# A Transformer expert layer: the products of v and W of two pairs taken together in seven block products

## The chip, the cores and the metric

The kernel runs on one core of a Trainium2 chip. The metric is the device time of one execution in microseconds. The engines are named as in the profile: PE (matrix products, with PEld for loading their stationary operand), DVE (vector engine), ACT (scalar engine, functions of one operand), POOL (GpSimd) and SP (here only a queue that issues DMAs). PE writes its results to eight PSUM banks of 512 columns of fp32; DVE and ACT read them there. Everything is in fp32.

## The reference, cut to what matters

x has 8 rows (batches) of 512 tokens of 256 values; each row has 64 context vectors and one anchor vector.

```python
nx = layer_norm(x, ln_gamma, ln_beta)
q = nx @ Wq
k = prototype_bank @ Wk
v = prototype_bank @ Wv
weights = softmax(einsum('bth,bph->btp', q, k) * H ** (-0.5))
evidence = einsum('btp,bph->bth', weights, v)
combined = concatenate([nx, evidence, anchor], axis=-1)        # 3 x 256 wide
router_probs = softmax(combined @ router_W + router_b)          # 3 experts
h = silu(einsum('btc,ecr->bter', combined, e_w1) + e_b1)        # 512 hidden values an expert
expert_out = einsum('bter,erh->bteh', h, e_w2) + e_b2
routed = sum(expert_out * router_probs[..., None], axis=-2)
g = sigmoid(silu(combined @ gate_w1 + gate_b1) @ gate_w2 + gate_b2)
return x + g * (routed @ out_w + out_b)
```

The kernel uses that `evidence @ W = weights @ (v @ W)`, where W is the middle third of an expert's first-layer weights. So it needs, for each row, the small product of v (64 x 256) and W (256 x 512 for each of three experts, and 256 + 2 columns for gate and router).

## The kernel before

The 8 rows are taken in 4 pairs, 0 to 3. A pair's two rows of v are stacked to 128 rows, so that one product of v and W serves both. A pair passes through three stages:

- `gate_layer(j, within)`: the first layer of the gate. Seven products of the two rows' x stand for eight (a block scheme after Strassen and Winograd, in which the two rows of a pair and the two halves of the contraction are the blocks). `within` is a table of further steps, run at named points (1, 5, 6, 3, "sums", 7, each after the product of that number).
- `half_layers(j)`: the first layers of the experts, written out by hand in `SLOTS` (pairs 1 to 3) and `SLOTS_0` (pair 0). A slot holds two half products, which run side by side on the two halves of PE's rows, and steps for other engines: `k` keeps a sum from PSUM, `a` adds one, `s` is silu, `w` weighs with the router's probabilities, `df` is a difference, `vw` the differences of v and W that the block scheme needs, `st`, `nm`, `lg`, `xd`, `xg` prepare x of the next pair.
- `outputs(j, between)`: the gate's second layer, then the second layers of the experts, again in block products (`experts`, six products of 512 columns each, into banks u, y, z), with `subtract` between them for the block differences and `keep` and `finish` to add the sums up. `finish` is three DVE operations (add the bank, multiply by the gate, transpose to `yb`), one POOL addition of x, and the stores on SP. `between` is a table of steps for the next pair, run at the points "begin", "gate", P1, P5, P6, P2, P7, P3, P4 in this order. Among these: `transpose_blocks` (x of one row by 32x32 blocks on DVE, then scaled on ACT), `scores` (PE), `exponents` (DVE, then eight exponentials on ACT), `combine_x` (four block differences of x, on POOL), `softmax`, `evidence_logits`, `router_logits` and `turn_weights` (DVE), `router_exp` (ACT).

The whole program is issued in the order in which it is written (`tc.manual_schedule(engines=None)`): each engine runs its instructions in that order, and waits are set where an operand, a tile or a bank is not yet free. So a step that is put at another point moves in every queue it uses.

`value_weights(j, g)` takes the product of v and W of pair j for expert g (or for gate and router, g = E): two products of 512 columns into a bank (L820), a copy by ACT into the tile `vw` (L827), and `value_differences` by DVE (L834, on 64 rows). In pairs 1 to 3 the steps stand at "begin" (gate and router), P6 (expert 2) and P7 (expert 0) of the outputs before, and at point 3 of the gate layer (expert 1, whose difference is the step `vw` in the half layers' first slot).

The block `pb` of router probabilities is spread over all rows by POOL's DMAs: four writes `pd` from the transposed probabilities to DRAM and one broadcast back (L800, L804), issued at the start of the half layers and first used by step `w00.2` in slot 17. The add behind it, `a10.2`, reads bank 5, into which slot 21 opens a new sum (`U.4`).

Lines that the text uses: L845 all products that go through `product`, L691 scores, L670 and L610 transposing and scaling of x, L682 `combine_x`, L705 to L719 `exponents` (L706 the copy of the first scores, L707 the clearing of them, L717 the maximum, L719 the exponentials), L735 and L736 `softmax`, L887 and L890 adding and keeping sums in the first layers, L921 and L924 `df` and `w`, L1300 `subtract`, L1330 to L1333 `finish` (L1333 is POOL's addition).

Of the kernel before, what the change touches and what calls it, by code (L numbers as in the profile page):

```python
# [8 lines left out]
F32 = mybir.dt.float32  # L9
AF = mybir.ActivationFunctionType  # L10
ALU = mybir.AluOpType
# [5 lines left out]
def kernel(  # L17
# [51 lines left out]
    nc = tc.nc  # L69
    P = 128  # L70
    B, T, H = x.shape
    CT = context.shape[1]
    E, C3, RH = e_w1.shape
    KH = H // P
# [7 lines left out]
    NP = B // 2  # L82
# [3 lines left out]
    const = ctx.enter_context(tc.tile_pool(name="const", bufs=1))  # L86
# [13 lines left out]
    def bank(i, name):  # L100
        ps = psum.tile([P, 512], F32, tag=f"b{i}", name=name)
        bank_of[ps.name] = i
        return ps
# [129 lines left out]
    w1 = const.tile([P, 2 * KH, R0 + ED], F32, tag="w1", name="w1")  # L233
# [53 lines left out]
    vT = const.tile([P, KH, B * CT], F32, tag="vT", name="vT")  # L287

    mr = const.tile([P, KH, B, CT], F32, tag="mr", name="mr")
# [206 lines left out]
    ow_sb = const.tile([P, KH, H], F32, tag="ow_sb", name="ow_sb")  # L496
# [79 lines left out]
    S = {}  # L576
# [47 lines left out]
    def logits(j):  # L624

        if ("lg", j) not in S:
            S["lg", j] = work.tile([P, E, NJ], F32, tag="lg", name=f"lg_{j}")
            nc.gpsimd.memset(S["lg", j][:, 0, :], 0.0)
        return S["lg", j]
# [70 lines left out]
    def exponents(j):  # L700
        ps = S.pop(("ps_s", j))
        w = work.tile([P, 2, NJ, TB], F32, tag="w", name=f"w_{j}", bufs=1)
        S["w", j] = w
        tokens = w.rearrange("p g j c -> p j g c")
        nc.vector.transpose(w.rearrange("p g j c -> p (g j c)"), ps)  # L705
        nc.vector.tensor_copy(logits(j)[:, 1, :], w[:, 0, :, 0])  # L706
        nc.vector.memset(w[:, 0, :, 0], 0.0)  # L707
        mx = work.tile([P, NJ], F32, tag="mx", name=f"mx_{j}")
        nc.vector.tensor_reduce(mx, tokens, AX.XY, ALU.max)
        sm = work.tile([P, NJ], F32, tag="sm", name=f"sm_{j}")  # L710
        S["sm", j] = sm
        if j == 0:
            nc.vector.tensor_tensor(w, w, by_token(mx), ALU.subtract)
            nc.scalar.activation(w, w, AF.Exp, scale=SCALE)
            return
        nmx = work.tile([P, NJ], F32, tag="nmx", name=f"nmx_{j}")
        nc.vector.tensor_scalar_mul(nmx, mx, -SCALE)  # L717
        for t in range(NJ):
            nc.scalar.activation(  # L719
                w[:, :, t, :], w[:, :, t, :], AF.Exp, bias=nmx[:, t : t + 1], scale=SCALE,  # L720
                accum_out=sm[:, t : t + 1],
            )
# [6 lines left out]
    def by_token(a):  # L729
        return a.unsqueeze(1).unsqueeze(3).to_broadcast([P, 2, NJ, TB])  # L730
# [80 lines left out]
    def value_weights(j, g, copy=nc.scalar.copy, whole=True):  # L811


        if ("vw", j) not in S:
            S["vw", j] = work.tile([P, R0 + ED], F32, tag="vw", name=f"vw_{j}", bufs=1)
        n0, n1 = (g * RH, (g + 1) * RH) if g < E else (G0, R0 + ED)
        vw = S["vw", j][:, n0:n1]
        ps = misc(f"ps_vw_{j}_{g}")[:, : n1 - n0]
        for k in range(KH):
            nc.tensor.matmul(  # L820
                ps,
                vT[:, k, j * 2 * CT : (j + 1) * 2 * CT],
                w1[:, KH + k, n0:n1],
                start=(k == 0),
                stop=(k == KH - 1),
            )
        copy(vw, ps)  # L827
        if whole and g < E:
            value_differences(j, g)

    def value_differences(j, g):
        odd = S["vw", j][CT:, g * RH : (g + 1) * RH]
        odd = odd.rearrange("p (q i c) -> p q i c", i=2, c=P)
        nc.vector.tensor_tensor(odd[:, :, 0, :], odd[:, :, 0, :], odd[:, :, 1, :], ALU.subtract)  # L834

    GROUPS = (NE // 2, *range(NE // 2))
    U, Z, Y = {}, {}, {}
# [3 lines left out]
    def product(ps, lhsT, rhs, start=False):  # L843

        return nc.tensor.matmul(ps, lhsT, rhs, start=start, stop=True, skip_group_check=not start)  # L845
# [80 lines left out]
    def gate_layer(j, steps):  # L926
# [63 lines left out]
        "P7.4 Z.6 | s10.3 w11.3 k10.6",  # L990
        "P2.4 P1.5 | w10.3",
        "P4.3 P5.5 | df.1 k00.5 df.3",
        "U.3 P2.4 |",
        "P5.6 Z.5 | a00.4",
        "P6.5 P4.3 | s00.4 k11.6 w00.4",
        "P7.6 Z.4 | s01.3",
        "P5.5 P6.5 | w01.3",
        "P2.5 P7.6 | k10.5 k11.5",
        "Y.5 P3.6 | a11.6",
        "Y.6 P7.4 | s11.6 w11.6",  # L1000
        "P7.5 P5.4 |",
        "P4.6 V.5 |",
        "P5.4 P7.5 |",
        "U.6 P3.5 | k11.4 a11.5",
        "P2.6 V.6 | a11.4 s11.5 s11.4 w11.5",
        "P3.5 P2.5 | w11.4",
# [92 lines left out]
    def half_layers(j):  # L1099
# [23 lines left out]
        def half(token, k):  # L1123
# [12 lines left out]

        b0 = 2 * j + 2
        simple = {
            "vw": lambda: value_differences(j, 1),
            "r": lambda: (router(j), spread_probabilities(j)),  # L1140
            "xb0": lambda: load_x_blocks(2 * j),
            "xb1": lambda: load_x_blocks(2 * j + 1),
# [8 lines left out]
            **{f"l{e}": lambda e=e: load_second(e) for e in range(1, E)},  # L1151
            **{f"t{u}": lambda u=u: transpose_second(u) for u in range(2 * E)},
        }
        ahead = {
            "dev": lambda: [deviation(j + 1, i) for i in range(2)],
            "xd0": lambda: store_x(b0),
# [78 lines left out]
    def outputs(j, steps):  # L1235
# [20 lines left out]
        t2, t3, t4 = gate_sums.pop(j)  # L1256
        g1, g2, g22 = scratch_x("r11"), scratch_x("r12"), scratch_x("r22")
        u, z, y = (bank(i, f"ps_g{n}_{j}") for n, i in (("u", 0), ("z", 2), ("y", 4)))
# [33 lines left out]
        def subtract(dst, other):  # L1292

            (k, i), (k2, i2), (k3, i3) = dst, *other
            for e in range(E):
                d, p, m = (
                    S["h", ii, e].rearrange("p (q k) t -> p q k t", k=2)[:, :, kk, :]
                    for kk, ii in ((k, i), (k2, i2), (k3, i3))
                )
                nc.vector.tensor_tensor(d, p, m, ALU.subtract)  # L1300
# [14 lines left out]
        def keep(r, ps):  # L1315
            nc.vector.tensor_tensor(r, r, ps, ALU.add)
# [42 lines left out]
        u, y, z = (bank(i, f"ps_{n}2_{j}") for i, n in ((1, "u"), (3, "y"), (5, "z")))  # L1359
# [5 lines left out]
        experts(z, combo(S1), 0, 1, start=True)  # L1365
        subtract((0, 1), ((1, 1), (0, 1)))
        keep(r22, z)
        subtract((0, 0), ((0, 1), (0, 0)))
        run("P5")
        experts(u, combo(S2), 0, 1)  # L1370
# [52 lines left out]
        y = work.tile([P, NT, P], F32, tag="yb", name="y_rows")  # L1423
# [4 lines left out]
    with tc.manual_schedule(engines=None):  # L1428
# [84 lines left out]
        for j in range(NP):  # L1513


            within, between = {}, {}

            def put(where, n, step, *args):
                where.setdefault(n, []).append(lambda: step(*args))

            spares(7, 5)
            if j == 0:
                spares(4, 5, 1)
                copies = []

                def value_product(g):
                    value_weights(0, g, lambda *args: copies.append(args), False)

                def copy_values():
                    nc.scalar.copy(*copies.pop(0))  # L1530

                put(within, 1, value_product, 0)
                put(within, 1, begin_softmax)
                put(within, 5, copy_values)
                put(within, 6, load_table, AF.Silu)
                put(within, 3, value_product, 1)
                put(within, 3, copy_values)
                put(within, "sums", end_softmax)
                put(within, 7, value_product, 2)
                put(within, 7, copy_values)  # L1540
                put(within, 7, end_setup)
            else:
                put(within, 3, value_weights, j, 1, nc.scalar.copy, False)
            if j + 1 < NP:
                b0, b1 = 2 * j + 2, 2 * j + 3
                if j + 2 < NP:
                    put(between, "begin", load_x, b0 + 2)
                    put(between, "begin", load_x, b1 + 2)
                put(between, "begin", transpose_blocks, b0)
                put(between, "gate", regroup_x, b1)  # L1550
                put(between, "begin", value_weights, j + 1, E)
                put(between, "begin", store_router_rows, j + 1)
                put(between, "begin", spread_router_rows, j + 1)
                put(between, "P5", transpose_blocks, b1)
                put(between, "P6", value_weights, j + 1, 2)
                put(between, "P2", scores, j + 1)
                put(between, "P2", exponents, j + 1)
                put(between, "P2", combine_x, j + 1, nc.gpsimd)
                put(between, "P7", softmax, j + 1)
                put(between, "P7", value_weights, j + 1, 0)  # L1560
                put(between, "P7", evidence_logits, j + 1)
                put(between, "P7", router_logits, j + 1)
                put(between, "P3", turn_weights, j + 1)
                put(between, "P3", router_exp, j + 1)
            gate_layer(j, within)
            half_layers(j)
            outputs(j, between)


# [32 lines left out]
```

## Time and profile before

| | |
|---|---|
| median of 3 runs (lowest to highest) | 457.83 us (457.56 to 457.87) |
| profiled execution, its time | 456.89 us |
| its span | 455.0 us |
| gate layer of pair 1, half layers | from 142.3, from 149.3 us |
| outputs of pair 1 | 198.4 to 247.0 us |
| gate layer of pair 2, half layers | from 247.0, from 254.0 us |
| outputs of pair 2 | 303.1 to 351.7 us |
| gate layer of pair 3, half layers | from 351.7, from 358.7 us |
| outputs of pair 3 | from 407.8 us |

In the profile an instruction's line names the line of the kernel, the engine and operation, what it writes and reads (`out<-in`, by the program's names), the shape and how many are merged. In a timeline the first two columns are start and duration in microseconds; a bracket at the end gives the time for which the engine had been idle before it and which instruction ended that idle time. Products overlap in their records: the duration of one is longer than the distance to the next, so the distance between starts is what a product costs. A product of fp32 shows as two records.

### The profile page before, as it was taken

The page shows a single profiled execution, that of the slowest core. Times are in us where ns is not written, and L with a number is a line of the kernel's source. Part 1 is how long each engine was busy: PE and PEld are TensorE (multiplying, and loading weights), DVE is VectorE, ACT ScalarE, POOL GpSimd, SP SyncE. Part 2 cuts the span into 40 slices and gives each one's busy share as a digit, 9 for nine tenths or more (in the row PEclk, how much of TensorE's full clock was granted, in tenths as well). Part 3 has the DMA queues.
Part 4 walks back from the last instruction along what each step waited for, and adds up shares of the span by engine and source line. Part 5 has one row for each costly group of instructions (what it writes and reads, how often), then busy time and mean ns, then how long its engine had stood idle before and what let it go on. Part 6 is the DMA issues. An engine that isn't in the chain of part 4 may idle for free.

```text
span 455.0 us, 5502 instructions
## 1 busy us (share of the span) xinstructions
PE 450.1 (99%) x1797; PEld 214.5 (47%) x1797; DVE 360.2 (79%) x683; ACT 214.0 (47%) x373; POOL 99.1 (22%) x149
## 2 busy tenths in 40 slices
PE   8999999999999999999999999999999999999996
PEld 7544445754444444444444444444444444444445
DVE  2878999949599899579699999479879747677983
ACT  3545875563221675466221576468220446558000
POOL 6466600252081300001072300001053400000010
PEclk9999999999999999999999999999999999999999
DMA  8984672354012477203011277002011381000014
GB/s 263 385 165 122 95 250 34 61 123 50 1 23 39 107 192 141 57 0 47 7 23 23 48 239 125 8 1 46 7 23 23 55 208 18 1 0 0 1 17 75
DMA packets 119379, 35.31 MB, mean 78 GB/s; under 512 B 106012, under 2 KB 116312, under 8 KB 118840
## 3 DMA queue, kind: packets, MB, share of 16 engines
q1 hardware_dynamic: 115344, 27.02, 28.9%
q0 software_dynamic: 2080, 7.16, 4.7%
q10 hardware_dynamic: 1928, 0.80, 0.7%
q8 instruction: 14, 0.23, 0.2%
q14 instruction: 13, 0.11, 0.1%
HBM read 27.56 MB, written 7.39 MB: 77 GB/s over the span
## 4 chain that ended last, share of the span: by engine, by line
PE 98%; DMA 1%; ACT 0%; DVE 0%; ACTq 0%; issue 0%
PE ps_u L845 45%; PE ps_z L845 20%; PE ps_y L845 14%; PE ps_vw L820 5%; PE ps_gu L845 3%; PE ps_w2o L547 2%; PE ps_s L691 2%; PE ps_gz L845 2%; PE ps_tokens L845 1%; PE ps_v L356 1%; DMA scr_w<-in_L_xcond_Wk_dram 1%; PE ps_m L356 1%; PE ps_gy L845 1%; PE pt_x L619 0%; PE ps_kq L369 0%; PE ps_ar L456 0%
## 5 line engine op out<-in xcount | busy, mean ns | idle before, releaser
L845 PE MATMUL ps_u<-nxT,w 64*128 64x512 f32 (+1 forms) x208 | 96.5, 590 | 0.0
L924 DVE TENSOR_TENSOR h<-h,pb 128x512 f32<-128x512 f32 x96 | 62.6, 684 | 16.3 <-ACT h L881 11.1
L845 PE MATMUL ps_u<-h,w2o 128*128 128x512 f32 x144 | 64.2, 595 | 0.0
L881 ACT ACTIVATE h<-h,abias 128x512 f32<-128x512 f32 x72 | 49.1, 717 | 29.8 <-DVE h L887 29.8
L845 PE MATMUL ps_z<-wT,vw 64*128 64x512 f32 x104 | 52.3, 590 | 0.0
L845 PE MATMUL ps_y<-nxT,w 64*128 64x512 f32 (+1 forms) x104 | 51.6, 590 | 0.0
L845 PE MATMUL ps_z<-nxT,ws 64*128 64x512 f32 (+1 forms) x104 | 51.5, 591 | 0.0
L845 PE MATMUL ps_z<-T,ws 64*128 64x512 f32 (+1 forms) x104 | 51.5, 590 | 0.0
L1333 POOL TENSOR_TENSOR yb<-yb,xb 128x512 f32<-128x512 f32 x14 | 17.7, 1267 | 149.0 <-DVE yb L1332 131.9
L845 PEld LDWEIGHTS ps_u<-nxT,w 64*128 64x128 f32 (+1 forms) x208 | 37.5, 187 | 25.6 <-issue 23.1
L845 PE MATMUL ps_u<-T,ws 64*128 64x512 f32 (+1 forms) x104 | 49.4, 589 | 0.0
L845 PE MATMUL ps_u<-T,w 64*128 64x512 f32 x112 | 48.3, 589 | 0.0
L845 PE MATMUL ps_z<-h,w2s 128*128 128x512 f32 x96 | 42.5, 592 | 0.0
L845 PEld LDWEIGHTS ps_u<-h,w2o 128*128 128x128 f32 x144 | 27.0, 190 | 32.6 <-issue 30.9
L890 ACT COPY h<-ps_u 128x512 f32<-128x512 f32 x48 | 27.8, 580 | 22.7 <-PE ps_u L845 22.7
L1300 DVE TENSOR_TENSOR h<-h,h 128x1024 f32<-128x1024 f32 x24 | 34.3, 1484 | 0.0
L433 POOL DMA_DIRECT2D vrd<-vw x8 | 5.0, 629 | 114.2 <-ACT vw L827 111.6
L845 PEld LDWEIGHTS ps_z<-h,w2s 128*128 128x128 f32 x96 | 18.2, 190 | 23.0 <-issue 21.8
L845 PE MATMUL ps_u<-wT,vw 64*128 64x512 f32 x56 | 28.3, 594 | 0.0
L845 PE MATMUL ps_y<-wT,vw 64*128 64x512 f32 x56 | 28.2, 595 | 0.0
L820 PE MATMUL ps_vw<-w,vT 128*128 128x512 f32 (+1 forms) x64 | 26.7, 539 | 0.0
L845 PEld LDWEIGHTS ps_y<-nxT,w 64*128 64x128 f32 (+1 forms) x104 | 19.4, 187 | 13.1 <-issue 12.8
(231 smaller groups left out, 817.1 us busy)
## 6 DMA issues: line engine op xcount, KB each, us to landing
pb<-pd POOLq DMA_DIRECT2D x4, 1536.0 KB, 6.9
xb<-in_x_dram SPq DMA_DIRECT2D x64, 64.0 KB, 2.5
out_dram<-yb SPq DMA_DIRECT2D x56, 64.0 KB, 1.8
x<-in_x_dram SPq DMA_DIRECT2D x24, 128.0 KB, 2.9
xd<-x SPq DMA_DIRECT2D x24, 128.0 KB, 2.3
xg<-xd SPq DMA_DIRECT2D x48, 64.0 KB, 2.3
w<-in_L_xcond_e_w_dram SPq DMA_DIRECT2D x4, 512.0 KB, 7.4
scr_wa<-in_L_xcond_e_w_dram SPq DMA_DIRECT2D x3, 512.0 KB, 10.2
```

The costliest lines, as they stand in the source:

```text
L356: nc.tensor.matmul(ps, w_sb[:, k, m * P : (m + 1) * P], src[:, k, :], start=(k == 0), stop=(k == KH - 1))
L433: nc.gpsimd.dma_start(S["vrd", j][i].rearrange("e c -> c e"), S["vw", j][row_half(i), R0:])
L547: nc.tensor.matmul(ps[:, d * H : (d + 1) * H], w2["T"][u % 2][:, c : c + P], ow_sb[:, k, :], start=(k == 0), stop=(k == KH - 1),)
L691: nc.tensor.matmul(ps[side(i, h), g * NH : (g + 1) * NH], mr[:, k, 2 * j + i, g * TB : (g + 1) * TB], S["nxT", 2 * j + i][:, k, h * NH : ( ...
L820: nc.tensor.matmul(ps, vT[:, k, j * 2 * CT : (j + 1) * 2 * CT], w1[:, KH + k, n0:n1], start=(k == 0), stop=(k == KH - 1),)
L845: return nc.tensor.matmul(ps, lhsT, rhs, start=start, stop=True, skip_group_check=not start)
L881: nc.scalar.activation(h, h if src is None else src, AF.Silu, bias=abias[:, c, 2 * j + i : 2 * j + i + 1])
L890: nc.scalar.copy(chunk(n, i, d), part)
L924: nc.vector.tensor_tensor(h, h, S["pb", j][:, i, :, 2 * q // RC, :], ALU.mult)
L1300: nc.vector.tensor_tensor(d, p, m, ALU.subtract)
L1333: nc.gpsimd.tensor_tensor(yb, yb, S["xb", 2 * j + row][:, i, :], ALU.add)
```

## The change

The products of v and W of pairs 2 and 3 are no longer taken one pair at a time. v of the two pairs and W of two experts (or the two halves of one) are 2 x 2 blocks each, and seven products of blocks stand for eight. Part 0 takes experts 0 and 1 (512 columns a product) in the outputs of pair 1; part 1 takes the two halves of expert 2 (256 columns) in the gate layer of pair 2. Each part has four steps (`late_values`):

- first: product 1 into bank u, product 2 into bank y; ACT copies u to c11, DVE adds y;
- second: product 6 is added into u; ACT copies u to c12;
- third: product 7 is added into u, product 5 goes into z; ACT copies z to c22, DVE adds u to it;
- fourth: product 4 is added into u, ACT copies u to c21; product 3 is added into z, DVE adds z to c12; then `value_differences`.

c11 and c12 are columns of pair 2's `vw`, c21 and c22 those of pair 3, which now lies in the tile of the first-layer weights, `w1`, in the rows of W that are no longer needed. Part 0's steps stand at P5, P6, P7 and P3, after the steps that stood there, part 1's at points 1, 5, 6 and 7 of the gate layer.

The block differences are taken by DVE: those of W for part 0 in four slots of pair 1's half layers (`v0` to `v3`), those of v in another (`vs`), those of W for part 1 at P4 of pair 1's outputs, which is after the last `finish`. Their homes are tiles that are free by then (`ow_sb`, part of `mr`, parts of `vT`, of `w1`, and one new tile).

Besides, for all pairs: the second row's `transpose_blocks` moves from P5 to a new point P8, between the `keep` of z and the subtraction that stood behind it; `scores`, `exponents` and `combine_x` move from P2 to P6, ahead of what else stands there; from pair 1 on, the copy of the first scores in `exponents` is done by ACT instead of DVE. Pair 3's `value_differences` come at P7, P3 and in the first slot of its half layers; pair 2 has none in that slot.

```diff
-        nc.vector.tensor_copy(logits(j)[:, 1, :], w[:, 0, :, 0])
+        (nc.scalar.copy if j else nc.vector.tensor_copy)(logits(j)[:, 1, :], w[:, 0, :, 0])
...
-        if ("vw", j) not in S:
+        if ("vw", j) not in S and j > JS:
+            S["vw", j] = w1[:, KH, :]
+        elif ("vw", j) not in S:
...
+    JS = NP - 2
+    late_v = {}
+
+    def block_rows(n):
+
+        ctx_of = [slice((JS + i) * 2 * CT, (JS + i + 1) * 2 * CT) for i in range(2)]
+        v = [[vT[:, k, ctx_of[i]] for k in range(KH)] for i in range(2)]
+        free = [vT[:, k, i * P : (i + 1) * P] for k in range(KH) for i in range(2)]
+        if n is None:
+            (a11, a12), (a21, a22) = v
+            s1, s2, s4, s3 = free
+            for dst, p, m, op in (
+                (s1, a21, a22, ALU.add), (s2, s1, a11, ALU.subtract),
+                (s3, a11, a21, ALU.subtract), (s4, a12, s2, ALU.subtract),
+            ):
+                nc.vector.tensor_tensor(dst, p, m, op)
+            return None
+        return {
+            1: v[0][0], 2: v[0][1], 3: free[2], 4: v[1][1], 5: free[0], 6: free[1], 7: free[3],
+        }[n]
+
+    def block_columns(part):
+
+        if part not in late_v:
+            if part == 0:
+                c0, n = 0, RH
+                t4 = const.tile([P, RH], F32, tag="late_t4", name="late_t4")
+                late_v["t4"] = t4
+                ts = ow_sb.rearrange("p k n -> p (k n)"), mr[:, :, : B // 2, :], t4
+            else:
+                c0, n = 2 * RH, RH // 2
+                ts = ow_sb[:, 0, :], ow_sb[:, 1, :], late_v["t4"][:, :n]
+            w = [
+                [w1[:, KH + k, c0 + i * n : c0 + (i + 1) * n] for i in range(2)] for k in range(KH)
+            ]
+            late_v[part] = w, ts
+        return late_v[part]
...
+    def late_difference(part, n):
+        ((b11, b12), (b21, b22)), ts = block_columns(part)
+        t1, t2, t4 = (t.rearrange("p k b c -> p k (b c)") if len(t.shape) > 3 else t for t in ts)
+        dst, p, m = ((t1, b12, b11), (t2, b22, t1), (b12, b22, b12), (t4, b21, t2))[n]
...
+    def late_product(part, n, ps, start=False):
+
+        ((b11, b12), (b21, b22)), ts = block_columns(part)
+        t1, t2, t4 = (t.rearrange("p k b c -> p k (b c)") if len(t.shape) > 3 else t for t in ts)
+        rhs = {1: b11, 2: b21, 3: b22, 4: t4, 5: t1, 6: t2, 7: b12}[n]
+        product(like(ps, rhs), block_rows(n), rhs, start)
+
+    def late_homes(part):
+        (c0, n) = (0, RH) if part == 0 else (2 * RH, RH // 2)
+        first, second = S["vw", JS], w1[:, KH, :]
+        return [a[:, c0 + i * n : c0 + (i + 1) * n] for a in (first, second) for i in range(2)]
+
+    def late_values(part, banks):
+
+        n = RH if part == 0 else RH // 2
+        u, y, z = (bank(i, f"ps_late_{m}")[:, :n] for i, m in zip(banks, "uyz"))
+
+        def plus(dst, ps):
+            nc.vector.tensor_tensor(dst, dst, ps, ALU.add)
+
+        def first():
+            c11 = late_homes(part)[0]
+            late_product(part, 1, u, True)
+            nc.scalar.copy(c11, u)
+            late_product(part, 2, y, True)
+            plus(c11, y)
+
+        def second():
+            late_product(part, 6, u)
+            nc.scalar.copy(late_homes(part)[1], u)
+
+        def third():
+            c22 = late_homes(part)[3]
+            late_product(part, 7, u)
+            late_product(part, 5, z, True)
+            nc.scalar.copy(c22, z)
+            plus(c22, u)
+
+        def fourth():
+            late_product(part, 4, u)
+            nc.scalar.copy(late_homes(part)[2], u)
+            late_product(part, 3, z)
+            plus(late_homes(part)[1], z)
+            for g in (0, 1) if part == 0 else (2,):
+                value_differences(JS, g)
+
+        return first, second, third, fourth
...
-        "U.3 P2.4 |",
+        "U.3 P2.4 | v0",
...
-        "P2.5 P7.6 | k10.5 k11.5",
+        "P2.5 P7.6 | k10.5 k11.5 vs",
...
-        "P7.5 P5.4 |",
-        "P4.6 V.5 |",
-        "P5.4 P7.5 |",
+        "P7.5 P5.4 | v1",
+        "P4.6 V.5 | v2",
+        "P5.4 P7.5 | v3",
...
-            "vw": lambda: value_differences(j, 1),
+            "vw": lambda: [value_differences(j, g) for g in ((1,) if j < JS else () if j == JS else (2,))],
...
+        for n in range(4):
+            simple[f"v{n}"] = lambda n=n: late_difference(0, n) if j == JS - 1 else None
+        simple["vs"] = lambda: block_rows(None) if j == JS - 1 else None
...
         keep(r22, z)
+        run("P8")
         subtract((0, 0), ((0, 1), (0, 0)))
         run("P5")
...
-            else:
+            elif j < JS:
                 put(within, 3, value_weights, j, 1, nc.scalar.copy, False)
+            elif j == JS:
+                for point, step in zip((1, 5, 6, 7), late_values(1, (6, 5, 7))):
+                    put(within, point, step)
...
-                put(between, "P5", transpose_blocks, b1)
-                put(between, "P6", value_weights, j + 1, 2)
-                put(between, "P2", scores, j + 1)
-                put(between, "P2", exponents, j + 1)
-                put(between, "P2", combine_x, j + 1, nc.gpsimd)
+                put(between, "P8", transpose_blocks, b1)
+                put(between, "P6", scores, j + 1)
+                put(between, "P6", exponents, j + 1)
+                put(between, "P6", combine_x, j + 1, nc.gpsimd)
+                if j + 1 < JS:
+                    put(between, "P6", value_weights, j + 1, 2)
+                elif j + 1 == JS:
+
+                    def late_start():
+                        for point, step in zip(("P5", "P6", "P7", "P3"), late_values(0, (0, 2, 4))):
+                            put(between, point, step)
+
+                    put(between, "P1", late_start)
+                    for n in range(4):
+                        put(between, "P4", late_difference, 1, n)
                 put(between, "P7", softmax, j + 1)
-                put(between, "P7", value_weights, j + 1, 0)
+                if j + 1 < JS:
+                    put(between, "P7", value_weights, j + 1, 0)
+                elif j + 1 > JS:
+                    put(between, "P7", value_differences, j + 1, 0)
+                    put(between, "P3", value_differences, j + 1, 1)
```

More of the change, by code (lines that the diff above doesn't have):

```diff
@@ new lines, in like @@
+    def like(a, b):
+        return a.rearrange("p (k n) -> p k n", k=KH) if len(b.shape) > 2 else a
+    def late_difference(part, n):
+        ((b11, b12), (b21, b22)), ts = block_columns(part)
+        t1, t2, t4 = (t.rearrange("p k b c -> p k (b c)") if len(t.shape) > 3 else t for t in ts)
+        dst, p, m = ((t1, b12, b11), (t2, b22, t1), (b12, b22, b12), (t4, b21, t2))[n]
+        wide = next((a for a in (dst, p, m) if len(a.shape) > 2), dst)
+        nc.vector.tensor_tensor(like(dst, wide) if len(dst.shape) == 2 else dst,
+                                *(like(a, wide) if len(a.shape) == 2 else a for a in (p, m)), ALU.subtract)
```

## The prediction

> **What bounds the kernel now.** I read the page first: busy times and the chain that ended last.
>
> ```profile
> span 455.0 us, 5502 instructions
> PE 450.1 (99%) x1797; PEld 214.5 (47%) x1797; DVE 360.2 (79%) x683; ACT 214.0 (47%) x373; POOL 99.1 (22%) x149
> ...
> PE 98%; DMA 1%; ACT 0%; DVE 0%; ACTq 0%; issue 0%
> ```
>
> PE is the whole path. Then its timeline in the outputs of pair 1, with the gate layer of pair 2 behind it:
>
> ```profile
> 222.66 5.31 PE L845 MATMUL ps_y<-h,w2o 128*128 128x512 f32 x12
> 227.90 1.93 PE L691 MATMUL ps_s<-nxT,mr 128*32 128x256 f32 x32
> 229.76 5.42 PE L845 MATMUL ps_u<-h,w2o 128*128 128x512 f32 x12
> 235.02 1.88 PE L820 MATMUL ps_vw<-w,vT 128*128 128x512 f32 x4
> 236.74 5.31 PE L845 MATMUL ps_z<-h,w2s 128*128 128x512 f32 x12
> 241.88 5.31 PE L845 MATMUL ps_u<-h,w2o 128*128 128x512 f32 x12
> 247.03 1.02 PE L845 MATMUL ps_u<-nxT,w 128*128 128x512 f32 x2
> ```
>
> Each group starts where the one before it hands over: no wait. A product of 512 columns is two records, 0.86 us by the starts (5.15 for six); one of 258 columns 0.43 (0.87 for two in the chain of waits). So the change can win only PE work, and every wait it makes is paid in full. VectorE, in the same stretch, is not level with PE:
>
> ```profile
> 228.01 0.69 DVE L1330 TENSOR_TENSOR r<-r,ps_y 128x512 f32<-128x512 f32 x1 [3.69 <-PE ps_y L845]
> ...
> 232.83 5.63 DVE L1300 TENSOR_TENSOR h<-h,h 128x1024 f32<-128x1024 f32 x3
> ...
> 241.00 1.77 DVE L736 TENSOR_TENSOR w<-w,rs 128x512 f32<-128x512 f32 x1
> 242.81 0.42 DVE L834 TENSOR_TENSOR vw<-vw 64x256 f32<-64x256 f32 x1
> ...
> 251.50 0.69 DVE L1330 TENSOR_TENSOR r<-r,ps_u 128x512 f32<-128x512 f32 x1
> ```
>
> It idles 3.69 us before y, then runs without a gap to 253.7; it takes up the last sum u at 251.5, 4.4 us after PE ended it (247.1). Today nobody waits for that lag. Its cause is visible on POOL: adds with operands in SBUF on both engines take turns.
>
> ```profile
> 232.96 2.21 POOL L682 TENSOR_TENSOR T<-nxT,T 128x512 f32<-128x512 f32 x1
> ...
> 240.96 1.27 POOL L1333 TENSOR_TENSOR yb<-yb,xb 128x512 f32<-128x512 f32 x1 [1.38 <-DVE rs L735]
> ```
>
> Alone the three subtractions take 3.49 (217.73), beside POOL 5.63; `w*rs` 1.77 against 0.69 for a plain add.
>
> **The change part by part.** All sums are against the profiled execution (456.89 us, span 455.0, 1.9 around it); it lies 0.94 below the median of the runs (457.83), to which I add the difference.
>
> *PE work.* Before, pairs 2 and 3 take 2 x 3 x 2 = 12 products of 512 columns, 10.30 us. After: seven of 512 (6.01) and seven of 256 (about 3.01): 9.02. Saved: 1.28. The work moves too: outputs of pair 1 get 3 products more (+2.58), gate layer of pair 2 +1.29, outputs of pair 2 -3.44, gate layer of pair 3 -1.72.
>
> *Differences of W and v in the half layers of pair 1 (`v0` to `v3`, `vs`).* Four DVE ops of 128x512 (0.60 each back to back, by the pairs at L921), four of 128x128 (0.29 each at L1407). They fall into holes of 0.64, 1.03 and 2.15 us (180 to 191 us; the last ends "2.15 <-PE ps_u"); at most 0.2 us late, and the sums behind them free banks that are not reused there. Cost 0; without these holes 3.6 us of DVE work.
>
> *Second row's x at P8, scores at P6.* The x blocks land at 216.0 and P8 comes at 217.7; scales end about 220.0, before PE asks for scores (222.7 in pair 1). Scores, score work on DVE (230.09 to 232.83, 2.74) and POOL's combination go into DVE's idle time before y. DVE then loses on its tail: 2.74, 1.1 of the subtractions (only the yb add contends, 4.45 for 5.55) and 0.36 of L1331. In pair 0's outputs the difference of vw waits for the copy behind eight exponentials (2.75) and may hold y's sum 1.5 us; the chain saved above, 4.2, pays for it. PE: 0 in pair 0. The copy of the first scores to ACT takes a DVE copy of 0.89 and adds a wait DVE to ACT and back: DVE's memset must follow it; about 0.4 (ACT's small ops: 0.22), inside the same idle time.
>
> *The wait for c22, outputs of pair 1.* The fourth step's product 4 adds into bank u, which DVE must first have added to c22; in DVE's order that add stands behind softmax, evidence and router logits. From y on, DVE does: 18.83 us before (228.01 to 246.83, where the sum of z begins), less 2.74, 1.1, 0.36 and the 0.45 of a vw difference, plus 0.65 for the add: 14.8. PE meanwhile: u 5.15, two products 1.72, z 5.15: 12.0. With 0.11 from PE's end to DVE's start and as much back, PE waits 3.0. Uncontended (less 1.1 twice) it would be 0.8. Behind the waiting product stand the last experts product and the gate layer, all of PE.
>
> *The wait for t2, gate layer of pair 2.* The four differences for expert 2 (128x256, 0.42 by L834) are issued at P4, after the last finish. That finish starts 0.1 after u and lasts 2.14 (251.50 to 253.64); difference 0 takes 0.42; then POOL's yb add, ready 0.15 after the finish, has its turn of 1.13 (by the alternation at 232 to 239), and difference 1 ends 0.3 later: 4.17 after u with the hand-over. PE needs t2 in product 6, after two own products and two of 256: 2.59. Wait 1.6 (0.6 if POOL comes later). The two waits are coupled: without the first, DVE reaches the finish 2.2 late and the second is 3.7; together they lie between 3.7 and 4.7, or 1.4 when nothing contends. I take 4.6, as the races for the turn were lost by 0.04 us in all three boundaries of the trace (240.96 against 241.00 here).
>
> *Pair 3.* PE's outputs of pair 2 are 3.44 shorter and the gate layer 1.72; DVE's tail shrinks only 4.2. By the same walk (+104.7) turn_weights ends at 352.2 and the bank of u is read at 353.3, when the half layers start (353.4): 0. But DVE is free 1.3 us after that start, before 0.35 ahead of it, and its vw difference meets POOL's yb, so the router's probabilities come 1.7 later:
>
> ```profile
> 366.61 0.56 POOL L804 DMA_DIRECT2D pb<-pd  x1 [3.36 <-DMA pd<-prT]
> ```
> ```profile
> 374.68 0.69 DVE L924 TENSOR_TENSOR h<-h,pb 128x512 f32<-128x512 f32 x1 [4.24 <-DMA pb<-pd]
> ```
>
> Here DVE waits for their broadcast, and the add behind it (a10.2, ends 375.97) frees bank 5 for slot 21, about 376.8: 0.8 us of cover, so 1.7 late costs 0.9. Lower end 0, upper 1.3.
>
> *Queues and the rest.* SP's issues keep their order; yb stores move with their finish. POOL's combination now stands before the first yb, done by about 227 against y at 230.8: free. ACT copies fall from six of 0.58 to four and four shorter.
>
> Sum: -1.28 + 3.0 + 1.6 + 0.9 = +4.2; 462.0 us.
>
> *Rules weighed.* The trace's turn for `w*rs` costs 1.1 over a plain add. [...] In the half layers before, PE goes on in banks other than the one that ACT or DVE reads, and waits nowhere. [...]
>
> **The rivals.**
> *Hidden anyway, a gain.* DVE runs late work by readiness, not in written order: then c22's add is done when its product is (about 238), t2 before the finish's wait for u, and both waits go: -1.28 with 0 to 0.9 of pair 3, 456.6 to 457.5. It decides if c22's add ends by 242.7. Against it: the vw difference at 242.81 ran where it is written though its copy had ended at 237.52.
> *Half the waits.* POOL's adds miss DVE's: 0.8 and 0.6 of wait, pair 3 0 to 0.9: 458.0 to 458.9; up to 460 if one of three contests stays. For it: the margin of 0.04. Against: three of three.
> *A new wait on W.* c21, c22 and t3 are written into the tile w1 that every first-layer product reads. If such products waited for these writes, gate and half layers of pair 2 would wait for DVE once or twice more, 1 to 2 us each: 463 to 466. Against it: POOL writes differences into the same tile in pair 0 and PE never waits there.
> *The saving is not there* if 256 columns cost as 512: 7 x 0.43 more, 465. Excluded by 0.43 a product of 258.
>
> **How the numbers follow.** Forecast (both waits, 460 to 463.3): 0.70. Half the waits: 0.15. Gain: 0.07. New wait on W: 0.08. I predict 462.0. From 458.5 to 463.6 lies the forecast, most of the half case and the near end of the last. A change under 0.2% (0.92 us) can't be told from none. Faster: 0.07; within it: 0.07, the near part of the half case; slower: 0.86.
>
> **What would show it.** PE starts with gaps of about 3 us before the fourth late product of part 0, 1.6 us before the third late product of part 1, under 1 us in slot 21 of pair 3, and nowhere else; between y's end and c22's add some 14.8 us of DVE without idle. I am wrong if DVE is at the c22 add by 12 us after y, or if the second difference for expert 2 ends before PE has ended its second gate product.

## The result and the profile after

The changed kernel takes 462.70 us (median of 5, 462.06 to 463.05) against 457.83 (5 runs, 456.27 to 457.91): ratio 1.0113, 95% interval 1.0095 to 1.0131. It is slower, by 4.9 us between the medians; 462.0 was predicted, with 458.5 to 463.6 as the range.

The page of the kernel after, in its first lines, the clock granted to PE (`PEclk`, in tenths of full speed) in 40 slices of the span, and the chain that ended last:

```profile
span 461.2 us, 5521 instructions
PE 451.3 (98%) x1801; PEld 215.5 (47%) x1801; DVE 368.7 (80%) x698; ACT 214.5 (47%) x378; POOL 99.7 (22%) x149
...
PEclk9999999999999999999998999999999999999999
...
PE 89%; DVE 5%; DMA 3%; POOL 1%; issue 0%; SPq 0%; DVEq 0%; POOLq 0%
```

PE was 98% of the chain and is now 89%, DVE has 5% of it, and one slice has a lower clock. The three longest waits of PE alone (us in total, times, longest):

```profile
PE ps_late_u L944 <- DVE w L907: 2.9, 1, 2.9
PE ps_late_u L944 <- DVE ow_sb L886: 1.5, 1, 1.5
PE ps_wake L316 <- DVE warm_t L195: 1.1, 1, 1.1
```

The third is in the trace of before too. The first two are new, and are those of the prediction: L907 is the line of DVE's additions of a bank, here of bank u to c22; L886 is a difference of W, here t2 for expert 2. PE's timeline around them:

```profile
236.50 1.02 PE L944 MATMUL ps_late_u<-w,vT 128*128 128x512 f32 x2
237.35 1.02 PE L944 MATMUL ps_late_z<-ow_sb,vT 128*128 128x512 f32 x2
238.21 5.31 PE L944 MATMUL ps_z<-h,w2s 128*128 128x512 f32 x12
246.46 1.41 PE L944 MATMUL ps_late_u<-late_t,vT 128*128 128x512 f32 x2 [2.94 <-DVE w L907]
247.67 1.91 PE L944 MATMUL ps_late_z<-w,vT 128*128 128x512 f32 x2
249.38 5.92 PE L944 MATMUL ps_u<-h,w2o 128*128 128x512 f32 x12
255.13 1.02 PE L944 MATMUL ps_u<-nxT,w 128*128 128x512 f32 x2
255.99 0.59 PE L944 MATMUL ps_late_u<-w,vT 128*128 128x256 f32 x2
256.42 0.59 PE L944 MATMUL ps_late_y<-w,vT 128*128 128x256 f32 x2
256.86 1.02 PE L944 MATMUL ps_z<-T,ws 128*128 128x512 f32 x2
259.41 0.67 PE L944 MATMUL ps_late_u<-ow_sb,vT 128*128 128x256 f32 x2 [1.53 <-DVE ow_sb L886]
```

DVE in the same stretch, and the two of POOL's additions that it meets:

```profile
231.55 0.69 DVE L1432 TENSOR_TENSOR r<-r,ps_y 128x512 f32<-128x512 f32 x1 [3.24 <-PE ps_y L944]
...
240.34 1.77 DVE L736 TENSOR_TENSOR w<-w,rs 128x512 f32<-128x512 f32 x1
...
245.73 0.68 DVE L907 TENSOR_TENSOR w<-w,ps_late_u 128x512 f32<-128x512 f32 x1
...
257.47 0.38 DVE L886 TENSOR_TENSOR ow_sb<-w 128x256 f32<-128x256 f32 x1
257.89 1.37 DVE L886 TENSOR_TENSOR ow_sb<-w,ow_sb 128x256 f32<-128x256 f32 x1
```
```profile
240.31 1.27 POOL L1435 TENSOR_TENSOR yb<-yb,xb 128x512 f32<-128x512 f32 x1 [4.37 <-DVE rs L735]
...
257.63 1.35 POOL L1435 TENSOR_TENSOR yb<-yb,xb 128x512 f32<-128x512 f32 x1 [7.75 <-DVE yb L1434]
```

DVE ends the addition to c22 at 246.41 and the second difference at 259.26; PE goes on 0.05 and 0.15 us later. The late products cost what was expected, 0.86 us for 512 columns (236.50 to 237.35) and 0.43 for 256 (255.99 to 256.42). What was not: after the first wait the product `ps_late_z`, two records, takes 1.71 us (247.67 to 249.38) where 0.86 is usual. The windows view shows why; its columns are the stretch, its length, the busy time of PE, PEld, DVE, ACT and POOL, the granted clock and the DMA:

```profile
243.80:247.20 3.40, 0.74 (x2) 0.49 (x3) 3.16 (x9) 0.22 (x1) 0.00 (x0) 1.00 0.15 26
247.20:250.60 3.40, 3.40 (x5) 1.35 (x4) 3.23 (x7) 0.58 (x1) 1.27 (x1) 0.50 0.00 0
250.60:254.00 3.40, 3.40 (x9) 1.49 (x8) 1.80 (x4) 0.00 (x0) 0.00 (x0) 1.00 0.45 77
```

For 3.4 us, from 0.7 us behind the wait, the clock is half: five product records instead of nine. PE does 1.7 us less work in it, so that is what it costs.

The difference of the two profiled executions, split at the points where the outputs of pairs 1, 2 and 3 begin (198.42, 303.12, 407.82 before; 199.04, 314.30, 414.06 after): up to pair 1's outputs +0.62, most of it before any changed instruction (an input lands later, and a gap ends at 67.4); from there to pair 2's outputs +10.56; to pair 3's outputs -4.94; the rest 0. The sum is the +6.2 between the spans. The +10.56 is 3.87 of moved work, 3.1 and 1.7 for the two waits by the starts (3.53 and 2.13 from the last product record's start before the wait to the first one's behind it, less the 0.43 that a record takes), 1.7 of slow clock and a rest of 0.2. The -4.94 is -5.16 of moved work and 0.2 of small gaps at the start of pair 3.

### The profile page after: what moved, and what is told of

Same layout as the page of the kernel before. It is cut to its first block, busy times and chain, and to the rows that moved or that the text cites. A ratio compares the mean times of both kernels' runs of the same rounds, so it can differ in the third digit from the quotient of the medians.

```text
span 461.2 us, 5521 instructions
## 1 busy us (share of the span) xinstructions
PE 451.3 (98%) x1801; PEld 215.5 (47%) x1801; DVE 368.7 (80%) x698; ACT 214.5 (47%) x378; POOL 99.7 (22%) x149
## 4 chain that ended last, share of the span: by engine, by line
PE 89%; DVE 5%; DMA 3%; POOL 1%; issue 0%; SPq 0%; DVEq 0%; POOLq 0%
PE ps_u L944 40%; PE ps_z L944 18%; PE ps_y L944 13%; PE ps_gu L944 3%; PE ps_vw L822 3%; PE ps_w2o L547 2%; DMA pb<-pd 2%; PE ps_s L691 2%; PE ps_gz L944 1%; PE ps_tokens L944 1%; PE ps_late_u L944 1%; DMA scr_ctx<-in_ctx_dram 1%; DVE h L1402 1%; PE ps_v L356 1%; PE ps_m L356 1%; PE ps_gy L944 1%
## 5 line engine op out<-in xcount | busy, mean ns | idle before, releaser
L1435 POOL TENSOR_TENSOR yb<-yb,xb 128x512 f32<-128x512 f32 x14 | 20.7, 1481 | 138.4 <-DVE yb L1434 125.3
L944 PE MATMUL ps_z<-wT,vw 64*128 64x512 f32 x78 | 39.2, 590 | 0.0
L1402 DVE TENSOR_TENSOR h<-h,h 128x1024 f32<-128x1024 f32 x24 | 37.4, 1611 | 0.0
L944 PEld LDWEIGHTS ps_z<-T,ws 64*128 64x128 f32 (+1 forms) x104 | 19.2, 187 | 12.5 <-issue 11.3
L944 PEld LDWEIGHTS ps_z<-nxT,ws 64*128 64x128 f32 (+1 forms) x104 | 19.0, 187 | 12.7 <-issue 9.8
L944 PEld LDWEIGHTS ps_u<-T,ws 64*128 64x128 f32 (+1 forms) x104 | 18.4, 187 | 13.2 <-issue 12.3
L944 PEld LDWEIGHTS ps_u<-T,w 64*128 64x128 f32 x112 | 18.3, 187 | 13.0 <-issue 12.3
```

The costliest lines, as they stand in the source:

```text
L1435: nc.gpsimd.tensor_tensor(yb, yb, S["xb", 2 * j + row][:, i, :], ALU.add)
```

## The experiments

The theory: the loss is two waits of PE for DVE, of which one brings a slow clock with it; both come of where DVE's steps stand in its order, not of too much DVE work. Rivals: DVE has too much work altogether, so that a wait only changes its place; the moved scores cost part of it; the slow clock has another cause.

The expected times are worked out from 462.7 us. The runs come from three chips, and the kernel before, run beside them, took not 457.83 us but 457.23 (both_early, c22_early, t2_early, fill3), 457.10 (order_only, products_only, fill1) and 457.02 (late_pb, both_early_2). So 0.6 to 0.8 us of a difference from an expected time can come of that; the ratios to before, taken on the same chip, are free of it.

### Both DVE steps earlier (both_early, both_early_2)

```diff
                         for point, step in zip(("P5", "P6", "P7", "P3"), late_values(0, (0, 2, 4))):
                             put(between, point, step)
+                        between["P7"].insert(0, between["P7"].pop())
...
-                    for n in range(4):
-                        put(between, "P4", late_difference, 1, n)
...
                 put(between, "P3", router_exp, j + 1)
+                if j + 1 == JS:
+                    put(between, "P1", lambda: [put(between, "P3", late_difference, 1, n) for n in range(4)])
```

> Change against the kernel after: the third late step (with DVE's add of u to c22) runs ahead of the softmax instead of behind the router logits, and the four differences for expert 2 are issued at P3, behind the fourth late step and ahead of the last finish, instead of at P4. Theory A (the loss is the two waits of PE for DVE and the slow clock behind the first): both waits go, no granted clock below 1.0, only the saved products stay: before less 1.1 to 1.3 us, about 456.6. Rival (DVE is simply too late as a whole, so a third wait takes their place, at the start of pair 2's half layers, for the bank of the last finish or for the turned weights): 457.5 to 460.

Measured: 455.99 us (11 runs) against 457.23 on the same chip, ratio 0.9975 (0.9965 to 0.9984). No wait on DVE is left after the setup, and the clock is full (mean 1.000 in the profiled run, 0.998 to 1.000 in all 11): in PE's timeline product 4 follows z at once, and product 6 of part 1 starts 0.1 us late.

```profile
236.96 5.31 PE L944 MATMUL ps_z<-h,w2s 128*128 128x512 f32 x12
242.11 1.02 PE L944 MATMUL ps_late_u<-late_t,vT 128*128 128x512 f32 x2
...
250.70 1.02 PE L944 MATMUL ps_z<-T,ws 128*128 128x512 f32 x2
251.66 0.67 PE L944 MATMUL ps_late_u<-ow_sb,vT 128*128 128x256 f32 x2
```

DVE does the same instructions as in the kernel after. It is only their order that made them late.

> The kernel both_early again, beside late_pb on the same chip: 0.25% below before, PE without a gap over 0.6 us after the setup.

On another chip, beside the last experiment below: 456.66 (10 runs) against 457.02, ratio 0.9988 (0.9978 to 0.9998). So this version is faster than both kernels; by how much it beats the kernel before is less certain, 0.1 to 0.25%, with 0.28% of PE work saved.

### One step at a time (c22_early, t2_early)

The first line of the diff above alone:

> Change against the kernel after: only the third late step moves ahead of the softmax. Theory A: the first wait (2.94) and the slow clock behind it (1.7) go, 4.8 less with the hand-over; but the finish of the last u now begins when DVE gets there (252.5 in the trace after), not when PE ends u, so the second wait grows from 1.5 to about 3.6: 459.9, or 461.6 if this wait is also followed by a slow clock. Rival (the waits are independent): second wait 1.5, 457.9.

Measured: 460.64 us (4 runs), ratio 1.0081 (1.0065 to 1.0096); the granted clock was 0.995 to 0.996 in the mean of each run. The first wait is gone and the second is twice as long:

```profile
251.01 1.02 PE L944 MATMUL ps_z<-T,ws 128*128 128x512 f32 x2
255.02 0.67 PE L944 MATMUL ps_late_u<-ow_sb,vT 128*128 128x256 f32 x2 [2.99 <-DVE ow_sb L886]
```

The waits are coupled, as the prediction had it (2.99 us of idle time, 3.15 by the starts, where it had 3.7). It is shorter because `w*rs` takes 1.18 instead of 1.77 in this order: it starts at 240.00, 0.63 us after POOL's addition (239.37), where it started beside it in the kernel after. And this longer wait, at another place and ahead of other products, is again followed by half the clock (0.51 from 255.7 to 259.1).

The other two parts of the diff alone:

> Change against the kernel after: only the four differences for expert 2 move to P3, into the 2.87 us in which DVE waits for the last u. Theory A: the second wait (1.53, 1.7 by the starts) goes, the first and the slow clock stay: 461.0. Rival (DVE is behind by the same work wherever it stands): 462.7.

Measured: 459.81 us (4 runs, 458.55 to 461.40), ratio 1.0065 (1.0041 to 1.0088). The second wait is gone; the first is as long as in the kernel after, 2.93. That should have left 461.0, or 460.4 with the 0.6 us by which before is faster here. What is still missing goes with the clock:

```profile
241.00:244.40 3.40, 1.54 (x4) 0.38 (x2) 3.15 (x7) 0.00 (x0) 0.00 (x0) 1.00 0.45 77
244.40:247.80 3.40, 2.33 (x6) 1.13 (x7) 3.21 (x7) 0.81 (x2) 0.17 (x1) 1.00 0.00 0
247.80:251.20 3.40, 3.40 (x10) 1.49 (x9) 3.26 (x8) 0.00 (x0) 1.09 (x1) 1.00 0.32 55
```

In the profiled run (458.55) the same wait, 242.5 to 245.5, brought no slow clock. Over the four runs the mean clock was 0.999, 0.996, 0.996 and 0.998; one stretch of 3.4 us at half clock makes 0.996. So the slow clock follows such a wait in some executions and not in others; the run without it is the fastest.

### The wait filled with products that nobody reads (fill3, fill1)

```diff
         def fourth():
+            if part == 0:
+                fill = bank(7, "ps_fill")
+                for _ in range(3):
+                    late_product(part, 3, fill, True)
             late_product(part, 4, u)
```

> Change against the kernel after: ahead of part 0's product 4 PE does three products of 512 columns into an unused bank, which nobody reads (2.57 us, inside the wait of 2.94). Product 4 starts when it did. Theory A1 (the slow clock, 0.62 granted over 4.5 us, comes of PE's idle time): no slow clock, 1.7 us less than after, 461.0. Rival A2 (it comes of something else, the late products themselves or this stage): granted clock as in the trace after, 462.7 or, if the fillers run slow too, more.

Measured: 461.17 us (4 runs), ratio 1.0086 (1.0069 to 1.0104), mean clock 0.999 to 1.000 in all four. Without the slow clock's 1.7 us the ratio would be 1.0076, which lies in the interval; the clock itself is the sharper sign. Product 4 starts 3.1 us after the end of z as in the kernel after, but at full speed:

```profile
238.69 5.31 PE L948 MATMUL ps_z<-h,w2s 128*128 128x512 f32 x12
243.84 2.74 PE L948 MATMUL ps_fill<-w,vT 128*128 128x512 f32 x6
246.94 1.13 PE L948 MATMUL ps_late_u<-late_t,vT 128*128 128x512 f32 x2 [0.36 <-DVE w L907]
247.90 1.02 PE L948 MATMUL ps_late_z<-w,vT 128*128 128x512 f32 x2
248.76 5.31 PE L948 MATMUL ps_u<-h,w2o 128*128 128x512 f32 x12
```

Here the slow clock comes of PE's idle time, not of the late products or of this stage: useless work in the same gap takes it away (0.36 us of idle time left; after, 2.94 and a mean clock of 0.996 in all five runs).

With `range(1)`:

> As fill3, but one product of 512 columns (0.86 us) instead of three, so that about 2.1 us of idle time stay ahead of product 4, between the 1.53 us that brought no slow clock and the 2.94 that did. If any idle time of 2 us and more brings it: granted clock near 0.62 for some 4 us as after, 462.7. If it takes more than 2.1 us: no slow clock, 461.0.

Measured: 461.19 us (4 runs, 460.79 to 462.75), ratio 1.0085 (1.0068 to 1.0103). The idle time was 2.08 us. In the profiled run (462.75, mean clock 0.996) the clock was half from 247.0 to 250.4; in the other three it was 1.00 and the times 460.8 to 461.5. Neither of the two expectations holds for all runs: an idle time of 2.1 us was enough in one execution and not in three.

### The moved steps alone, the joint products alone (order_only, products_only)

```diff
-    JS = NP - 2
+    JS = NP + 1
```

> The kernel after without the joint products: every pair takes its own twelve products a kernel before as before; the moved steps stay (second row's x at P8; scores, exponents and combination at P6; first scores' copy on ACT). Theory A (moving them costs nothing, PE never waited there and does not now): 457.8, within 0.2% of before, PE without a gap over 0.3 us outside the setup. Rival (the moved scores cost part of the loss, by the wait DVE to ACT and back, or by the difference of vw behind the eight exponentials): 458.8 or more.

Measured: 456.80 us (11 runs) against 457.10, ratio 0.9997 (0.9988 to 1.0006). The moved steps cost nothing and bring nothing by themselves. The two things feared of them are there, and hidden. DVE in pair 0's outputs:

```profile
121.18 0.07 DVE L707 MEMSET w<- 128x8 f32 x1 [0.31 <-ACT lg L706]
...
125.68 0.42 DVE L836 TENSOR_TENSOR vw<-vw 64x256 f32<-64x256 f32 x1 [3.51 <-ACT vw L829]
126.13 0.69 DVE L1432 TENSOR_TENSOR r<-r,ps_y 128x512 f32<-128x512 f32 x1
```

The memset waits 0.31 us for ACT's copy, the difference of vw 3.51 for the copy behind the exponentials, and the sum of y follows only then. DVE is late by it, PE is not.

```diff
-        (nc.scalar.copy if j else nc.vector.tensor_copy)(logits(j)[:, 1, :], w[:, 0, :, 0])
+        nc.vector.tensor_copy(logits(j)[:, 1, :], w[:, 0, :, 0])
...
-                put(between, "P8", transpose_blocks, b1)
-                put(between, "P6", scores, j + 1)
-                put(between, "P6", exponents, j + 1)
-                put(between, "P6", combine_x, j + 1, nc.gpsimd)
+                put(between, "P5", transpose_blocks, b1)
+                put(between, "P2", scores, j + 1)
+                put(between, "P2", exponents, j + 1)
+                put(between, "P2", combine_x, j + 1, nc.gpsimd)
```

> The kernel after with the joint products but with the moved steps put back (second row's x at P5; scores, exponents and combination at P2; first scores' copy on DVE). Theory A: the score work, 2.74 us, and the contended subtractions and multiply, 1.5, come back onto DVE's tail between y and the sum of c22, so the first wait grows from 2.9 to about 7.2, followed by the slow clock; second wait 1.5: about 467. Rival (the wait does not follow DVE's tail): 462.7.

Measured: 469.04 us (4 runs), ratio 1.0262 (1.0247 to 1.0278). The first wait was 5.08 us, not 7.2: the scores, 1.86 us of PE, stand behind y here, which the expectation forgot to take off. The clock was half over 6.8 us (246.8 to 253.6), of which the first 2.9 lie inside the wait, and two new waits came: 1.1 for ACT's copy of c11, now behind the later scaling of x, and 0.9 of idle time at the start of pair 3's half layers, 2.1 by the starts against both_early. So 467 was near by luck: the new waits stand for what the first one lacks. What holds is that the joint products need the moved steps, which took the idle time of PE from 8.6 us to 4.5.

### The router's probabilities of pair 3 made later (late_pb)

The prediction's 0.9 us in pair 3 did not come. Was it the mechanism, or its size?

```diff
+        for _ in range(4 if j == NP - 1 else 0):
+            nc.gpsimd.tensor_tensor(late_v["t4"], late_v["t4"], late_v["t4"], ALU.subtract)
         S["pb", j] = work.tile([P, 2, 2, E, NH], F32, tag="pb", name=f"pb_{j}", bufs=1)
```

> both_early with four POOL additions of 128x512 on an unused tile ahead of the broadcast of pair 3's router probabilities (about 5.1 us on POOL against the 2.05 to 2.7 it waits for the writes anyway), so that the broadcast is issued some 2.5 us later, about 11.4 us after the start of pair 3's half layers, and lands at about 18.7 instead of 16.2. Theory P (the prediction's: the add behind the first weighing frees bank 5 for slot 21, 18.1 us after that start): PE waits in slot 21, about 2.0 us (1.4 to 2.6 with the spread of the landing), 458.0. Rival (that bank, or that step, does not gate PE): no gap in slot 21, 456.0 as both_early.

Measured: 459.39 us (5 runs, 458.39 to 460.95), ratio 1.0056 (1.0034 to 1.0079), 2.7 us over both_early_2 on the same chip. In the profiled run (458.39) pair 3's half layers start at 358.36 and the broadcast lands at 376.82, 18.5 later (18.7 expected). DVE, then PE in slot 21:

```profile
376.91 0.69 DVE L1025 TENSOR_TENSOR h<-h,pb 128x512 f32<-128x512 f32 x1 [6.06 <-DMA pb<-pd]
377.52 0.68 DVE L988 TENSOR_TENSOR h<-h,ps_z 128x512 f32<-128x512 f32 x1
```
```profile
376.12 0.59 PE L946 MATMUL ps_z<-wT,w 64*128 64x512 f32 x1
378.26 0.69 PE L946 MATMUL ps_u<-nxT,w 64*128 64x512 f32 x1 [1.55 <-DVE h L988]
```

The mechanism holds: bank 5 is freed by the add behind the first weighing, and PE waits for it there, 1.7 us by the starts. The other 1 us of the median goes with the clock again: 0.999, 0.995, 0.996, 0.996 and 0.999 in the five runs, and the three slow-clock runs are the three slowest. How long PE waited in those three is not known: the landing of the broadcast spreads, and only the profiled run has a trace.

## Why the prediction was right, and where it was not

The mechanism was right: two waits of PE for DVE, at the products and of the sizes that were forecast. The number was right in part by luck. Between the two profiled executions the difference is 6.2 us, where the sum has 4.2. What it lacks is the slow clock (1.7), the later start (0.6) and 0.4 in the two waits and the rest; what it has too much is 0.7 in pair 3. The medians are only 4.9 us apart, since the profiled execution of before was 0.9 us faster than the median and that of after 0.35 slower. So 462.0 came within 0.7 of 462.7 because a missing term, a surplus one and the spread of the runs partly cancelled.

*The wait for c22* was priced at 3.0 and measured 2.94 of idle time (3.1 by the starts). The walk of DVE held in its parts: from the sum of y to the end of the add 14.86 us (231.55 to 246.41; predicted 14.8), with the subtractions at 4.45 (233.63 to 238.08; 4.45), `w*rs` at 1.77 beside POOL, and PE's 12.0. POOL's addition met DVE's `w*rs` as in the trace of before, 0.03 us ahead of it (240.31 against 240.34).

*The wait for t2* was priced at 1.6 and measured 1.53 (1.7 by the starts). The second difference ran into POOL's turn as said: 1.37 us where the first took 0.38. It ended at 259.26, 4.1 us behind u, where 4.17 was predicted. c22_early, in which DVE reads bank u ahead of the softmax, takes the first wait away and hands it on, as the prediction said: the second is 2.99 there, where it had 3.7. The 460.6 us of that run lie between the 459.9 and the 461.6 expected of it: the slow clock of the 461.6 came, the second wait was 0.6 shorter and before was 0.6 faster beside it, which leaves 460.4.

*The saved PE work and the moved steps* are as predicted: 0.86 and 0.43 us a product, nothing for the moved scores (order_only) and nothing for the differences in the half layers of pair 1, where PE has no gap.

*Pair 3* failed in size: 0.9 predicted, 0.2 measured, in three gaps of some 0.07 us (363.8, 364.3 and 370.1) and not in slot 21. The step that failed is "so 1.7 late costs 0.9". In the kernel after, pair 3's half layers start at 364.86, and DVE has:

```profile
368.65 0.21 DVE L797 STREAM_TRANSPOSE prT<-pr 128x32 f32<-128x32 f32 x1
...
381.20 0.69 DVE L1023 TENSOR_TENSOR h<-h,pb 128x512 f32<-128x512 f32 x1 [4.53 <-DMA pb<-pd]
```

Counted from that start, the probabilities were ready 1.75 us later than before, as walked (3.99 against 2.24), but their broadcast landed only 0.35 later (16.24 against 15.89). The way from ready to landed, writes, wait and broadcast, took 13.65 us in the one execution read before, and 12.25 after, 11.6 to 12.5 in c22_early, t2_early, fill3 and both_early. It is a DMA time that spreads by some 2 us (11.3 in products_only to 13.65), taken from its longest sample. late_pb shows that the gate itself is there.

*Missing* was the slow clock, 1.7 us of the result: no term of the sum had it, and the trace of before could not show it, since PE never waits there after its setup.

The rivals: a gain by readiness fell (both DVE steps ran where they are written). The rival of half the waits fell too: POOL met DVE again at each of the contests, `w*rs` among them. A new wait on W is not seen: after the setup PE's only waits over 0.2 us are the two. That DVE is too late as a whole, which the prediction's word of a "tail" suggests, fell with both_early.

## What to carry to other kernels

When one engine is the whole path, judge a change by the order of the engines that feed it: here the same DVE instructions cost some 6 us in one order and nothing in another. For each new read of a bank between two products into it, count the engine's queue from the last thing it waited for to that read, and PE's work over the same stretch; move what PE waits for ahead of what it does not. In a kernel like this one, a wait of 2 to 3 us on PE should be priced with a slow clock behind it (here 1.7 us, in some or all executions), and a DMA's landing time taken from several executions.

## What the runs showed of the hardware

Half the clock after a wait of PE was not expected. In the traces it comes in stretches of 3.413 us by the trace's record of the granted clock (247.2 to 250.6 after, 247.0 to 250.4 in fill1, 255.7 to 259.1 in c22_early) or two of them (246.8 to 253.6 in products_only), and begins 0.6 to 0.8 us after the end of the three single waits. In the same record, the time at full clock before it is 242.3, 242.3, 249.2 and 242.3 us, which is 71, 71, 73 and 71 times 3.413. The time at full clock behind it in the kernel after is 211.6 us, 62 times 3.413; in the kernel before it is 450.6 us, 132 times, to a drop behind the last instruction. So the changes in these traces fall on a fixed raster of such stretches that does not move with the wait. By that raster, the stretch before a slow one had PE busy for 0.7 us of 3.4 (after), 1.3 (fill1), 0.7 (c22_early), and 1.2 and 0.5 (products_only); in t2_early the wait of 2.93 lay across two stretches, with 1.5 and 2.3 busy, and the clock stayed. Over the runs a mean clock of 0.995 to 0.996 stands in 5 of 5 with an idle time of 2.94 (after; the idle times are those of the profiled runs), 4 of 4 with 2.99 (c22_early), 2 of 4 with 2.93 (t2_early), 1 of 4 with 2.08 (fill1) and none of 4 with 1.53 and 0.36 (fill3); and in 3 of 5 of late_pb, whose wait was 1.55 in the profiled run, at full clock, and is not known in the others. The length of the wait alone does not decide: 2.08 had a slow clock behind it and 2.93 had none. If the share of busy time in such a stretch decides, the limit lies between 39% (1.3 of 3.4 us, fill1, slow) and 45% (1.5 of 3.4, t2_early, not slow). That is an estimate from these few traces; no run varied the share by itself.
